# An attention kernel's last batch: output of the batch ahead in an earlier slot, partial products in later slots, a short chunk's products in column blocks

## The chip, the cores and the metric

The kernel runs on one core of a Trainium2 chip. The core has five engines with a queue of instructions each: TensorE (PE, matrix products; its weight loads are shown apart as PEld), VectorE (DVE), ScalarE (ACT), GpSimd (POOL) and SyncE (SP), which issues DMAs. An engine takes its instructions in the order in which the program gives them, and an instruction that waits holds up all behind it on the same engine. DMAs are issued by SP, ACT or POOL and are carried out by 16 DMA engines. The metric is the time of one execution on the device in microseconds (us).

## The reference

The input `x` has 8 batches of 512 features by 1024 tokens, and `cond_2048` is a mask of zeros and ones over the tokens, about half of each. Queries, keys and values are the same projection `q`. The output is `x` plus the attention's result:

```python
xt = jnp.transpose(x, (0, 2, 1))
q = xt @ Wq.T
qh = q.reshape(B, T, NH, dk).transpose(0, 2, 1, 3)
scores = scale * jnp.einsum('bhqd,bhkd->bhqk', qh, qh)
logits = (scores * cmask + (1.0 - cmask) * NEG) * rmask
attn = jax.nn.softmax(logits, axis=-1)
ctx = jnp.einsum('bhqk,bhkd->bhqd', attn, qh)
ctx = ctx.transpose(0, 2, 1, 3).reshape(B, T, D)
out = ctx @ Wo.T
return jnp.transpose(out, (0, 2, 1))      # and x is added to it
```

There are 8 heads of 64 features. `cmask` is the mask over keys, `rmask` over queries. A masked key has no weight. A masked query has all its logits at zero, so its result is the mean of the values of all tokens, the same for every masked query of a batch.

## The kernel before

The kernel computes only with the kept tokens of a batch. `NK` = 544 rows hold the kept tokens and, as the last row, the mean of all tokens, which stands for every masked query. (Were more tokens kept, another version of the same code with 576 rows, or one without the selection, would run; neither does here.) The 544 rows are cut into five chunks: four of 128, and a short one, number `LAST` = 4, of 32 (`END`). `sizes[i]` is a chunk's row count and `places[i]` its rows in the result: the short chunk's are 0 to 31, chunk 0's 32 to 159, and so on.

Work goes by pairs of heads: 4 pairs a batch, 32 in all, written (b, pr) below. The loop over `pairs` (lines 1302 to 1381) writes the order out by hand, in five slots k = 0 to 4 a pair. Each slot takes one chunk of keys, the short one first (`order`, line 1276). In a slot stand, in this order: the chunk's scores (`scores`: products on PE, exponentials on ACT); at slot 0 the contexts of an earlier pair; fetches of an earlier batch (`fetch`, on POOL, each after a tiny copy `keep_step` that reads this slot's exponentials and so holds POOL back until then); the slot's tasks from `slots_of(p)`, which are projections, values, the attention of the pair before, and output products of the batch before; row loads (`load_rows`, on SP); and transposes of an earlier batch (`finish_blocks`, on VectorE). Tables such as `FETCH_LAST` say which pieces go into which (pr, k).

The names that the change touches:

- `output` (line 869) computes a chunk's result for all four pairs, has ACT copy it to `oc`, and stores it from POOL's queue into `od`, a buffer in memory with 544 rows a batch. For the short chunk it uses four column blocks already: the 512 columns are cut into four of 128, and each goes to another 32 partitions of the same bank, so that copy and store have 128 partitions.
- `load_rows`, `fetch` and `finish_blocks` turn that into the output. For each of 8 pieces, `load_rows` loads rows of `x` (turned, in the buffer `xd`) into `g`; `fetch` gathers the matching rows of `od` and has DMA add them to `g`; `finish_blocks` transposes `g` into `xr`. A fetch waits for all stores to the batch's `od`. After the eighth transpose `xr` is stored to the output in four DMAs of 512 KB on SP's queue (line 949). For batches 0 to 5 this happens two batches on; for batch 6, in pairs (7,2) and (7,3).
- `inverses`, `spread`, `contexts`: the reciprocals of the sums of exponentials. `inverses` works them out on VectorE, `spread` brings them to all rows by products on PE and a copy on ACT, and `contexts` multiplies a pair's result `cT` by them on VectorE. For all but the last two pairs, `invert` does the spreading by DMAs (`row`, `rb`).
- The last batch has no batch behind it that could hide its output. `begin_output` (line 893) forms a chunk's product of the first three pairs during the last pair (7,3) and copies it to `pa`. After the loop, `attend_last` ends the last pair, and `end_output` (line 909) adds the fourth pair's product, a chunk at a time, and stores the sum into `od` from SP. Then `fetch_last` gathers eight pieces of 128 tokens on POOL (line 958), and `finish_tokens` transposes each on PE (line 987), adds `x` on VectorE (line 988) and stores 256 KB from ACT's queue. The gather of piece i waits for the stores of the short chunk and of chunks 0 to i.

Of the kernel before, what the change touches and what calls it, by code (L numbers as in the profile page):

```python
# [13 lines left out]
ALU = mybir.AluOpType  # L14
# [292 lines left out]
def attention_of_kept_tokens(ctx, tc, x, mask, wq, wo, out, ident, wqT, woT, verdict, flag):  # L307


    nc = tc.nc  # L310
    B, D, T = x.shape
    P = 128
    DK = D // NH
    SCALE = 1.0 / math.sqrt(DK)
    ND = D // P
# [4 lines left out]
    A = P // Q  # L320
# [570 lines left out]
    partials = {}  # L891

    def begin_output(b, i):

        n = sizes[i]
        po = bank(f"pa_{b}_{i}")
        for pr in range(ND - 1):
            nc.tensor.matmul(
                po[:n, :],
                cTs[b, pr][:, i * P : i * P + n],  # L900
                woT[:, pr, :],
                start=(pr == 0),
                stop=(pr == ND - 2),
            )
        pa = sb.tile([P, D], F32, tag="xin", name=f"pa_{b}_{i}", bufs=NC)
        nc.scalar.copy(pa[:n, :], po[:n, :])
        partials[i] = pa

    def end_output(b, i):
        n = sizes[i]  # L910
        if i == 0:
            ods[b] = dr.tile([NK, D], F32, tag="od", name=f"od_{b}")
        po = bank(f"po_{b}_{i}")
        nc.tensor.matmul(
            po[:n, :],
            cTs[b, ND - 1][:, i * P : i * P + n],
            woT[:, ND - 1, :],
            start=True,
            stop=True,
        )  # L920
        oc = sb.tile([P, D], F32, tag="oc", name=f"oc_{b}_{i}", bufs=NC)
        nc.vector.tensor_tensor(
            oc[:n, :].rearrange("p (d a f) -> p a d f", d=ND, a=A),
            po[:n, :].rearrange("p (a d f) -> p a d f", d=ND, a=A),
            partials[i][:n, :].rearrange("p (a d f) -> p a d f", d=ND, a=A),
            ALU.add,
        )
        nc.sync.dma_start(ods[b][places[i], :], oc[:n, :])

# [71 lines left out]
    def slots_of(p):  # L1001
# [7 lines left out]
        def do(k, f, *args):  # L1009
            todo[k].append(lambda: f(*args))  # L1010
# [60 lines left out]
        elif ahead:  # L1071
            do(1, project_with_values)
            do(2, lengths_of, behind)
            do(2, end_attend, before)
            do(3, project_with_top, 1)
        elif behind:
            do(1, output, b - 1, LAST - 1)
            do(1, values, behind)
            do(2, lengths_of, behind)
            do(2, end_attend, before)  # L1080
            do(3, bias_of, behind)
            do(3, output, b - 1, LAST)
        if p == ND - 1:
# [173 lines left out]
    def late(n):  # L1257
# [39 lines left out]
        FINISH = {(0, 4): (0, 1), (1, 1): (2, 3), (1, 2): (4, 5), (1, 4): (6, 7)}  # L1297
        FETCH_LAST = {(2, 4): (0, 1, 2), (3, 0): (3, 4, 5), (3, 1): (6, 7)}
        FINISH_LAST = {(3, 1): (0, 1, 2), (3, 2): (3, 4, 5), (3, 3): (6, 7)}
        ROWS = {(2, 2): (0, 1), (2, 3): (2, 3), (3, 0): (4, 5), (3, 2): (6, 7)}  # L1300
        ROWS_LAST = {(2, 0): (0, 1, 2), (2, 1): (3, 4, 5), (2, 2): (6, 7)}
        for p, pair in enumerate(pairs):
# [3 lines left out]
            for k, c in enumerate(order):  # L1306
# [78 lines left out]
        attend_last(last)  # L1385
        for i in (0, LAST, *range(1, LAST)):
            end_output(B - 1, i)
# [116 lines left out]
```

## Time and profile before

| | us |
|---|---|
| median of 3 runs | 659.57 |
| lowest and highest | 658.69 to 660.84 |
| the profiled execution | 660.24 |
| its span, first to last instruction | 658.5 |
| PE busy | 618.8 (94%) |
| ACT busy | 383.6 (58%) |
| DVE busy | 355.7 (54%) |
| POOL busy | 212.0 (32%) |
| mean granted TensorE clock | 0.980 |

The profile is of one execution. In its timeline a row has the start in us, the duration, the engine, the line of the kernel, the operation, out<-in by the program's names with shapes, and a count of merged instructions; in square brackets stands the time for which the engine was idle before, and what ended it. A matmul with 32-bit operands shows as two records. In the rows by stretches stand, after the stretch and its length, the busy time and count of PE, PEld, DVE, ACT and POOL, then the granted TensorE clock, the DMA engines' mean busy share, and GB/s.

Pair (7,2) runs in the profiled execution from about 578 to 598 us, pair (7,3) from there to about 620, `attend_last` to 628, the last products to 633, and the gathers and final stores to the end.

### The profile page before, as it was taken

Reading aid. Unit: us, or ns where it says so; the run is one execution under the profiler, and the core shown is the slowest. Engines: PE = TensorE matmul, PEld = TensorE weight load, DVE = VectorE, ACT = ScalarE, POOL = GpSimd, SP = SyncE. Lnnn points to the kernel's source line nnn. Section 1 sums busy time; section 2 is a strip of 40 time slices with the busy share of each in tenths; the row PEclk is TensorE's granted clock in tenths of the full one; section 3 lists DMA queues with packets and bytes.
Section 4 is the critical chain, followed back from the end, with each engine's and each line's share of the span. In section 5 each row is a group of like instructions: output and inputs, shape, how many; then the busy total and the mean of one; then the engine's idle time right before and its main releaser. Section 6 shows DMA issues by size and latency. Waiting matters only on the chain. (4 is left out here: it accounts for less than half of the span.)

```text
span 658.5 us, 15960 instructions
## 1 busy us (share of the span) xinstructions
PE 618.8 (94%) x6092; PEld 383.9 (58%) x6092; DVE 355.7 (54%) x1032; ACT 383.6 (58%) x1020; POOL 212.0 (32%) x313
## 2 busy tenths in 40 slices
PE   5799799999999999999999999999999999998963
PEld 4765476656665666556665666566665666554422
DVE  5545566434475666746475548565665425435542
ACT  4268558755766567754776577655775466553400
POOL 5620500150067003830166004720275006205331
PEclk9999899999999999999999999999999999999975
DMA  8556622354488657977599666975795636477776
GB/s 244 176 199 162 222 69 66 113 193 132 134 177 218 231 176 191 189 242 228 169 180 274 196 189 151 205 249 180 200 174 156 196 102 102 101 178 179 123 219 195
DMA packets 94542, 116.61 MB, mean 177 GB/s; under 512 B 11911, under 2 KB 61639, under 8 KB 94462
## 3 DMA queue, kind: packets, MB, share of 16 engines
q1 hardware_dynamic: 74030, 75.20, 38.6%
q0 software_dynamic: 16208, 38.25, 25.1%
q10 hardware_dynamic: 4224, 2.10, 1.1%
q8 instruction: 49, 0.80, 0.5%
q14 instruction: 31, 0.25, 0.1%
HBM read 72.81 MB, written 42.70 MB: 175 GB/s over the span
## 5 line engine op out<-in xcount | busy, mean ns | idle before, releaser
L687 ACT ACTIVATE e<-s,bias 128x544 f32<-128x544 f32 x256 | 180.5, 710 | 73.6 <-PE s L679 60.2
L679 PE MATMUL s<-qT 64*64 64x272 f32 x2048 | 155.0, 398 | 5.5 <-ACT e L687 3.8
L743 PE MATMUL av<-e,v 64*64 64x272 f32 x1920 | 132.2, 392 | 0.0
L593 PE MATMUL pq<-xc,wqT 128*128 128x272 f32 x512 | 131.3, 401 | 0.0
L593 PEld LDWEIGHTS pq<-xc,wqT 128*128 128x128 f32 x512 | 93.3, 190 | 36.9 <-issue 20.6
L679 PEld LDWEIGHTS s<-qT 64*64 64x64 f32 x2048 | 77.3, 133 | 54.8 <-ACT e L687 12.4
L878 PE MATMUL po<-woT,cT 128*128 128x512 f32 (+1 forms) x448 | 108.9, 439 | 0.0
L889 POOL DMA_DIRECT2D od<-oc x56 | 30.2, 544 | 236.5 <-ACT oc L887 235.7
L972 POOL DMA_INDIRECT g<-od,block_origin x56 | 90.1, 1610 | 29.4 <-DVE ends L716 8.3
L743 PEld LDWEIGHTS av<-e,v 64*64 64x64 f32 x1920 | 76.5, 134 | 38.1 <-issue 2.1
L659 DVE TENSOR_REDUCE m<-pq 128x1 f32<-128x128 f32 x28 | 8.2, 292 | 136.4 <-ACT qT L605 111.9
L878 PEld LDWEIGHTS po<-woT,cT 128*128 128x128 f32 (+1 forms) x448 | 46.5, 149 | 54.6 <-issue 53.2
L603 ACT COPY qT<-pq 128x272 f32<-128x272 f32 x64 | 24.6, 385 | 69.5 <-PE pq L650 28.2
L942 DVE STREAM_TRANSPOSE xr<-g 128x512 f32<-128x512 f32 x56 | 58.0, 1101 | 7.1 <-DMA g<-od,block_origin 7.1
L640 DVE TENSOR_REDUCE len<-sq 128x10 f32<-128x640 f32 x32 | 25.7, 804 | 59.2 <-ACT sq L638 59.2
L969 POOL COPY step<-e 1x1 f32<-1x1 f32 x75 | 24.0, 320 | 96.5 <-ACT e L687 96.4
L687 ACT ACTIVATION_READ_ACCUMULATOR e<-s,bias 128x1 f32 x256 | 50.5, 197 | 0.0
L539 POOL DMA_INDIRECT xin<-xd,source x40 | 39.1, 978 | 16.0 <-DMA woT<-in_L_cond_Wq_dram 5.8
L887 ACT COPY oc<-po 128x512 f32<-128x512 f32 (+1 forms) x35 | 18.0, 515 | 44.0 <-PE po L878 43.1
L493 ACT ACTIVATE junka<-x 128x512 f32<-128x512 f32 x56 | 35.2, 629 | 1.3
L474 DVE STREAM_TRANSPOSE xt<-x 128x1024 f32<-128x1024 f32 x28 | 34.8, 1241 | 0.7 <-issue 0.2
L527 DVE TENSOR_SCALAR_CACHE_REDUCE junk<-rank,key 128x1024 f32<-128x1024 f32 (+4 forms) x35 | 34.9, 997 | 0.0
(174 smaller groups left out, 674.6 us busy)
## 6 DMA issues: line engine op xcount, KB each, us to landing
xd<-xt SPq DMA_DIRECT2D x120, 128.0 KB
x<-in_x_dram SPq DMA_DIRECT2D x56, 256.0 KB
g<-xd SPq DMA_DIRECT2D x56, 256.0 KB
out_dram<-xr SPq DMA_DIRECT2D x28, 512.0 KB
rb<-row SPq DMA_DIRECT2D x60, 160.0 KB
od<-oc POOLq DMA_DIRECT2D x28, 256.0 KB
rank<-ranks SPq DMA_DIRECT2D x6, 512.0 KB
x<-in_x_dram POOLq DMA_DIRECT2D x8, 256.0 KB
```

The lines of the kernel that those rows point to most:

```text
L474: nc.vector.transpose(xt.rearrange("p k (d f) -> p k d f", d=ND), xs[b][r][:, :, at : at + n].rearrange("p d (k t) -> p k d t", t=Q),)
L493: nc.scalar.activation(junk, xs[b][r][:, d, :], AF.Copy, accum_out=xbars[b][:, d, r : r + 1])
L527: nc.vector.tensor_scalar(junk[:, :n], rank[:, i * P :], key[:, col], 0.0, ALU.is_le, ALU.add, accum_out=found[:, col])
L539: nc.gpsimd.indirect_dma_start(out=xin[:n, :], out_offset=None, in_=xds[b], in_offset=bass.IndirectOffsetOnAxis(ap=searches[b][2][:n, i : ...
L593: nc.tensor.matmul(pq[:, :KH], wqT[:, d, pr * P : (pr + 1) * P], xcs[b][:, d, cols], start=(d == 0), stop=(d == ND - 1),)
L679: nc.tensor.matmul(ss[h][r * DK : (r + 1) * DK, hf, :KH], qT[heads[h], c * P + r * DK : c * P + (r + 1) * DK], qT[heads[h], queries[hf]], ...
L687: nc.scalar.activation(e[:, :, h, :], ss[h][:, :, :KH], AF.Exp, bias=bias, scale=SCALE, accum_out=sums[pair[1] % 2][:, h, c : c + 1],)
L743: nc.tensor.matmul(avs[pair][hf][head, :KH], v[keys, c, head], e[keys, hf, h, :], start=(c == 0 and not crossed), stop=(c == LAST - 1 and ...
L878: nc.tensor.matmul(po[k * n : (k + 1) * n, :w], cTs[b, pr][:, i * P : i * P + n], woT[:, pr, k * w : (k + 1) * w], start=(pr == 0), stop=( ...
L889: nc.gpsimd.dma_start(ods[b][places[i], k * w : (k + 1) * w], oc[k * n : (k + 1) * n, :w])
L942: nc.vector.transpose(xr.rearrange("p (d a) (t i) -> p a d t i", a=A, i=NT)[..., i], gs[b, i].rearrange("p (a d f) -> p a d f", a=A, f=Q),)
L972: nc.gpsimd.indirect_dma_start(out=gs[b, i], out_offset=None, in_=ods[b], in_offset=bass.IndirectOffsetOnAxis(ap=block_origin[:, b, i : i ...
```

## The change

Three things change together, all of them around the last batch:

1. In pair (7,2) the last two output products of batch 6, chunks 3 and `LAST`, both go to slot 0 (before: slots 1 and 3). The tables for batch 6 move with them: row loads from slots 0 to 2 of (7,2) to slots 2 to 4 of (7,1) and slot 1 of (7,2); fetches from (7,2) slot 4 and (7,3) slots 0 and 1 to (7,2) slots 2 to 4 and (7,3) slots 0 and 1, at most two a slot; transposes from (7,3) slots 1 to 3 to (7,2) slot 4 and (7,3) slots 1 and 2.
2. In the last pair, `spread` and `contexts` of the pair before go to slot 0 (before: slot 1), and the five partial products to slots 1, 2, 3, 4, 4 (before: 1, 1, 2, 3, 4).
3. The short chunk of the last batch uses four column blocks too, in `begin_output` and `end_output`. The blocks take the columns of `woT` in the final order, so the add needs no reordering for it. It becomes the first chunk of the last five, and its store four DMAs, two each from SP and ACT.

```diff
+    def add_product(b, i, pr, po, start, stop):
+
+        n = sizes[i]
+        parts = P // n
+        w = D // parts
+        tokens = cTs[b, pr][:, i * P : i * P + n]
+        if parts == 1:
+            nc.tensor.matmul(po, tokens, woT[:, pr, :], start=start, stop=stop)
+            return
+        in_order = woT[:, pr, :].rearrange("p (a d f) -> p d a f", a=A, d=ND)
+        for k in range(parts):
+            nc.tensor.matmul(
+                po[k * n : (k + 1) * n, :w],
+                tokens,
+                in_order[:, k * ND // parts : (k + 1) * ND // parts, :, :],
+                start=start,
+                stop=stop,
+            )
+
     def begin_output(b, i):
...
         for pr in range(ND - 1):
...
+            add_product(b, i, pr, po, pr == 0, pr == ND - 2)
+        w = D // (P // sizes[i])
         pa = sb.tile([P, D], F32, tag="xin", name=f"pa_{b}_{i}", bufs=NC)
-        nc.scalar.copy(pa[:n, :], po[:n, :])
+        nc.scalar.copy(pa[:, :w], po[:, :w])
         partials[i] = pa
 
     def end_output(b, i):
...
-        if i == 0:
+        if i == LAST:
             ods[b] = dr.tile([NK, D], F32, tag="od", name=f"od_{b}")
         po = bank(f"po_{b}_{i}")
...
+        add_product(b, i, ND - 1, po, True, True)
         oc = sb.tile([P, D], F32, tag="oc", name=f"oc_{b}_{i}", bufs=NC)
...
+        else:
+            nc.vector.tensor_tensor(oc[:, :w], po[:, :w], partials[i][:, :w], ALU.add)
+        for k in range(parts):
+            queue = nc.scalar if k % 2 else nc.sync
+            queue.dma_start(ods[b][places[i], k * w : (k + 1) * w], oc[k * n : (k + 1) * n, :w])
...
         elif behind:
-            do(1, output, b - 1, LAST - 1)
+            do(0, output, b - 1, LAST - 1)
+            do(0, output, b - 1, LAST)
             do(1, values, behind)
             do(2, lengths_of, behind)
             do(2, end_attend, before)
             do(3, bias_of, behind)
-            do(3, output, b - 1, LAST)
...
             for i in range(NC):
-                do((1, 1, 2, 3, 4)[i], begin_output, b, i)
+                do((1, 2, 3, 4, 4)[i], begin_output, b, i)
...
-        FETCH_LAST = {(2, 4): (0, 1, 2), (3, 0): (3, 4, 5), (3, 1): (6, 7)}
-        FINISH_LAST = {(3, 1): (0, 1, 2), (3, 2): (3, 4, 5), (3, 3): (6, 7)}
+        FETCH_LAST = {(2, 2): (0, 1), (2, 3): (2, 3), (2, 4): (4, 5), (3, 0): (6,), (3, 1): (7,)}
+        FINISH_LAST = {(2, 4): (0, 1), (3, 1): (2, 3, 4), (3, 2): (5, 6, 7)}
         ROWS = {(2, 2): (0, 1), (2, 3): (2, 3), (3, 0): (4, 5), (3, 2): (6, 7)}
-        ROWS_LAST = {(2, 0): (0, 1, 2), (2, 1): (3, 4, 5), (2, 2): (6, 7)}
+        ROWS_LAST = {(1, 2): (0, 1), (1, 3): (2, 3), (1, 4): (4, 5), (2, 1): (6, 7)}
...
-                if p + 1 == len(pairs):
-                    if k == 1:
-                        spread(before, inv)
-                        contexts(before)
+                if p + 1 == len(pairs) and k == 0:
+                    spread(before, inv)
+                    contexts(before)
...
-        for i in (0, LAST, *range(1, LAST)):
+        for i in (LAST, *range(LAST)):
             end_output(B - 1, i)
```

More of the change, by code (lines that the diff above doesn't have):

```diff
@@ L891, in attention_of_kept_tokens @@
     partials = {}
+    def add_product(b, i, pr, po, start, stop):
[15 more added lines that the diff above has]
+            )
     def begin_output(b, i):
-        n = sizes[i]
         po = bank(f"pa_{b}_{i}")
         for pr in range(ND - 1):
[L898 to L904, printed above, removed]
+            add_product(b, i, pr, po, pr == 0, pr == ND - 2)
+        w = D // (P // sizes[i])
         pa = sb.tile([P, D], F32, tag="xin", name=f"pa_{b}_{i}", bufs=NC)
-        nc.scalar.copy(pa[:n, :], po[:n, :])
+        nc.scalar.copy(pa[:, :w], po[:, :w])
         partials[i] = pa
@@ L910, in end_output @@
         n = sizes[i]
-        if i == 0:
+        parts = P // n
+        w = D // parts
+        if i == LAST:
             ods[b] = dr.tile([NK, D], F32, tag="od", name=f"od_{b}")
         po = bank(f"po_{b}_{i}")
[L914 to L920, printed above, removed]
-        oc = sb.tile([P, D], F32, tag="oc", name=f"oc_{b}_{i}", bufs=NC)
[L922 to L928, printed above, removed]
+        add_product(b, i, ND - 1, po, True, True)
+        oc = sb.tile([P, D], F32, tag="oc", name=f"oc_{b}_{i}", bufs=NC)
+        if parts == 1:
+            nc.vector.tensor_tensor(
+                oc.rearrange("p (d a f) -> p a d f", d=ND, a=A),
+                po.rearrange("p (a d f) -> p a d f", d=ND, a=A),
+                partials[i].rearrange("p (a d f) -> p a d f", d=ND, a=A),
+                ALU.add,
+            )
+        else:
[3 more added lines that the diff above has]
+            queue.dma_start(ods[b][places[i], k * w : (k + 1) * w], oc[k * n : (k + 1) * n, :w])
     def in_blocks(t):
```

## The prediction

> **What bounds the kernel now.** I read the page first, then the chain that ended last, then the timeline of the last two pairs and of the tail, then busy time by stretches.
>
> ```profile
> span 658.5 us, 15960 instructions
> PE 618.8 (94%) x6092; PEld 383.9 (58%) x6092; DVE 355.7 (54%) x1032; ACT 383.6 (58%) x1020; POOL 212.0 (32%) x313
> ```
> ```profile
> 644.05 7.22 DMA g<-od,origin
> ...
> 651.40 1.10 PE o L987 x4
> ...
> 652.52 0.69 DVE x L988
> ```
>
> TensorE is busy for 94% of the span, so up to about 633 us a stall or a saving on PE counts one for one. After that PE is nearly empty, and the end hangs on the eight fetches of the last batch (POOL, line 958). Two things therefore set the end: when PE reaches the last products (line 914), and how long after them the first fetch starts.
>
> ```profile
> 620.42 1.12 DVE L942 STREAM_TRANSPOSE xr<-g 128x512 f32<-128x512 f32 x1 [0.60 <-DMA g<-od,block_origin]
> 620.51 1.14 PE L725 MATMUL av<-e,v 128*64 128x272 f32 x8
> 621.39 0.15 DVE L819 SCALAR_TENSOR_TENSOR share<-share,lacks,pads 128x4 f32<-128x4 f32 x1
> 621.56 5.29 SPq L949 DMA_DIRECT2D out_dram<-xr  x4
> 622.53 1.31 PE L805 MATMUL rb<-ident,ris 128*64 128x128 f32 x20 [0.89 <-DVE ris L826]
> 627.88 4.87 PE L914 MATMUL po<-woT,cT 128*128 128x512 f32 x10
> 628.48 0.15 DVE L796 COPY cT<-qT 128x1 f32<-128x1 f32 x1
> 629.77 4.07 SPq L928 DMA_DIRECT2D od<-oc  x5
> 630.02 0.68 DVE L922 TENSOR_TENSOR oc<-po,pa 32x512 f32<-32x512 f32 x1 [0.28 <-PE po L914]
> 635.22 1.00 POOL L958 DMA_INDIRECT g<-od,origin  x1 [19.14 <-DMA od<-oc]
> ```
>
> Batch 6's fetches and transposes (lines 972, 942) run through the last pair. Its last transpose stands on VectorE ahead of the last pair's inverses (line 819 on), so PE waits 0.89 us at the spread (line 805). Then batch 6's output, 4 x 512 KB, is issued on SP at 621.56, and the last batch's od stores queue behind it: the short chunk's add ends at 630.70, and the fetch that needs it and chunk 0 starts at 635.22, 4.5 us later.
>
> **The change part by part.** The sum is made against the profiled execution: 660.24 us, 1.7 over its span and 0.67 over the median of 659.57.
>
> *Short chunk in blocks.* Three matmuls with 512 moving columns become twelve with 128.
>
> ```profile
> 590.93 1.08 PE L878 MATMUL po<-woT,cT 128*32 128x128 f32 x32
> 617.81 2.76 PE L898 MATMUL pa<-woT,cT 128*32 128x512 f32 x6
> ```
>
> The rows count each f32 matmul twice. Line 878 has the blocked form already: 32 records in 1.08 us, 0.034 each. So 24 records cost 0.81 us where the partial product took 2.76: **-1.9 us** of PE (bounds -2.0, and -1.0 if the strided moving operand of line 914's new helper halves the rate). The copy to `pa` shrinks too, but nobody waits for it.
>
> *Order of the last products.* The short chunk now goes first, and it needs the last context column, ready at 628.63; before, chunk 0 ran under that wait. Its 8 records cost some 0.3 us and its 128x128 add some 0.2. By the old clock times: short chunk 628.9 to 629.3, chunk 0 to 630.1, add of chunk 0 630.2 to 630.9. So the later of the two stores that fetch 0 needs is released at 630.9, where it was 630.7: **+0.2** (bounds 0 and +0.8, one SP issue, 4.07 / 5). Of the short chunk's four stores two are on ACT's queue, which is idle there; the two on SP pass before chunk 0's add ends.
>
> *Batch 6's end moved ahead.* Its last six transposes now stand ahead of the inverses by two score blocks and more; by the times worked out below they end near 615, the inverses come near 619, and most of the 0.89 wait goes: **-0.8** (bounds -0.9 and 0). The output stores start there too. The old ones, issued at 621.56, still kept DMA at 0.92 and 0.88 between 630 and 634, some 12.4 us; the new ones are out at about 627.5.
>
> ```profile
> 630.00:632.00 2.00, 2.00 (x5) 0.97 (x6) 1.43 (x3) 0.00 (x0) 0.00 (x0) 1.00 0.92 199
> 632.00:634.00 2.00, 0.76 (x2) 0.01 (x1) 1.67 (x5) 0.00 (x0) 0.00 (x0) 1.00 0.88 274
> ...
> 654.00:656.00 2.00, 0.00 (x0) 0.00 (x0) 0.00 (x0) 0.00 (x0) 0.00 (x0) 0.50 0.49 139
> 656.00:658.50 2.50, 0.00 (x0) 0.00 (x0) 0.00 (x0) 0.00 (x0) 0.00 (x0) 0.50 0.00 0
> ```
>
> The last column but one is the DMA share. The kernel's very last 256 KB store meets empty queues: its add ends at 653.21 and DMA is silent from 656, at most 2.8 us. With 0.3 for POOL to start, the 4.5 us wait becomes 3.1: **-1.4** (bounds -1.9, and 0 if the wait isn't made by the queue). The next fetches don't wait: all adds end within line 914's 4.87 us, and POOL alone takes 1.00 for each fetch.
>
> *Contexts of the pair before at slot 0.* This takes out two PE waits of before (0.81 us for an exponential, 1.28 for the contexts), but only if VectorE delivers. And here the same change puts something in its way. Two of batch 6's transposes now stand at the end of pair (7,2), so on VectorE they are ahead of the contexts and inverses that the spread at slot 0 of (7,3) needs.
>
> ```profile
> 589.00:591.00 2.00, 1.46 (x25) 0.77 (x23) 0.98 (x2) 1.94 (x6) 0.00 (x0) 1.00 0.01 2
> ...
> 595.00:597.00 2.00, 2.00 (x17) 0.97 (x16) 1.72 (x6) 0.39 (x1) 0.00 (x0) 1.00 0.87 288
> ```
> ```profile
> 581.57 3.70 PE L878 MATMUL po<-woT,cT 128*128 128x512 f32 x8
> 581.74 0.71 ACT L687 ACTIVATE e<-s,bias 128x544 f32<-128x544 f32 x1 [1.51 <-PE s L679]
> 592.63 1.98 POOL L889 DMA_DIRECT2D od<-oc  x4 [5.90 <-ACT oc L887]
> 593.83 0.70 ACT L687 ACTIVATE e<-s,bias 128x544 f32<-128x544 f32 x1
> 594.17 0.23 DVE L854 TENSOR_TENSOR rb<-rb 128x64 f32<-128x64 f32 x1 [2.39 <-DMA rb<-row]
> 597.45 0.18 DVE L827 TENSOR_SCALAR ris<-ends,pads 128x2 f32<-128x2 f32 x1
> 599.84 1.13 PE L679 MATMUL s<-qT 64*64 64x272 f32 x12 [0.81 <-ACT el L704]
> 600.90 1.31 PE L805 MATMUL rb<-ident,ris 128*64 128x128 f32 x20
> 600.94 1.70 POOL L972 DMA_INDIRECT g<-od,block_origin  x1 [6.16 <-DVE ends L716]
> 602.94 1.58 POOL L972 DMA_INDIRECT g<-od,block_origin  x1 [0.25 <-issue]
> 605.40 3.70 PE L898 MATMUL pa<-woT,cT 128*128 128x512 f32 x8 [1.28 <-DVE cT L862]
> 605.85 1.11 DVE L942 STREAM_TRANSPOSE xr<-g 128x512 f32<-128x512 f32 x1 [0.31 <-DMA g<-od,block_origin]
> 608.14 1.11 DVE L942 STREAM_TRANSPOSE xr<-g 128x512 f32<-128x512 f32 x1 [1.18 <-DMA g<-od,block_origin]
> ```
>
> When is that spread, S, now? Batch 6's last products move to slot 0 of (7,2): they start a score block (1.1 us) earlier than 581.57, at 580.6, and end after 3.70 + 1.08 at 585.4; as before, 0.6 us later POOL issues the short chunk's four stores for 1.98, to 588.0. The first fetch needs them landed. Before, it started 6.3 us after their issue ended (594.61 to 600.94), but with DMA at 0.87 from other loads; the bound below is the 2.8 + 0.3 of the quiet store. The new place, 588 to 591, is quiet (0.01 at 589), because the row loads (line 936) have moved into pair (7,1), so I take the near end: fetch 0 at 591.1, fetch 1 two us on at 593.1. Fetches land 4.9 (600.94 to 605.85) and 5.2 us after their start; with `rb` and two row loads beside them, I take 5.5: fetch 1 is in at 598.6. Then one transpose, 1.1, contexts and inverses, 3.5 (594.17 to 597.63), and 0.1 to start: **S = 603.3** where it was 600.90. Bounds: 602.7, all of it quiet, and 606.8, with the 6.3 and a landing of 5.8.
>
> What runs behind S is as long as before: the partial products wait for the contexts 4.5 us after the spread starts (605.40 - 600.90), and spread 1.31, one score block 1.1 and two products 1.7 lie below that. So the term is S - 600.90 = **+2.4**, the two old waits included. VectorE ends the contexts at 607.8, adds the ends (1.0) and does the six transposes (6.7): 615.5. PE begins the last attention at 620.51 + 2.4 - 1.9 = 621.0; the exponentials that the inverses need lie a partial product (2.8 or less) before.
>
> *Filler lost in (7,2).* Both products now lie ahead of the score blocks, where they no longer cover the exponentials. The first exponential moves from 581.74 to about 586.6; four pairs of them at 1.5, the copies and the square (2.1) and some 1.3 of waits for scores bring the last one to 596.0 instead of 594.53. So PE is free for the spread at 600.4, not 599.0 (599.84 - 0.81): +1.4 (bounds 0 and +2.7), which lies wholly under the wait until 603.3, and costs itself if that wait is gone. SP only gains: six row loads now pass before batch 5's output (576.4), where VectorE, not the queue, is what that output waits for; two stay behind the `rb` loads. The other queue, POOL's, holds nothing but fetches there.
>
> Sum: +2.4 - 1.9 - 0.8 + 0.2 - 1.4 = -1.5, that is S - 604.8. 658.7 for the profiled execution, **658.1** as a median: a gain of 0.2%, inside the 0.3% (2 us) in which a measurement of this kernel can't tell a change from none.
>
> One thing speaks against it, the granted clock (third column from the end), here early in the span and after the last product:
>
> ```profile
> 70.00:75.00 5.00, 1.83 (x25) 0.91 (x17) 4.49 (x20) 0.83 (x3) 3.99 (x7) 1.00 0.73 224
> 75.00:80.00 5.00, 4.91 (x48) 2.54 (x48) 1.64 (x6) 3.59 (x9) 3.33 (x4) 0.66 0.38 134
> ...
> 631.95:635.36 3.41, 1.08 (x3) 0.08 (x1) 2.29 (x8) 0.00 (x0) 0.14 (x1) 1.00 0.92 314
> 635.37:638.00 2.63, 0.00 (x0) 0.00 (x0) 0.00 (x0) 0.00 (x0) 2.02 (x3) 0.50 0.38 134
> ```
>
> In the lower rows PE was busy for 1.08 of 3.41 us, and the clock fell from 1.00 to 0.50. In the upper ones PE was busy for 1.83 of 5 us, and then the mean was 0.66 over 5 us, that is half the clock for (1 - 0.66) / 0.5 x 5 = 3.4 us. The new wait at the spread is 603.3 - 600.4 = 2.9 us, nearly as empty. [...]
>
> **The rivals.**
> 1. *The hold on VectorE is short.* If the fetches land so early that S is between 600.4 (PE's own pace) and 602.8, the time is 655.2 to 657.6; middle 656.4. For it: the queues are empty at 589. Against: it needs fetch 1 landed by 598.1, under the bound from the rows.
> 2. *The hold is long; slower.* If fetch 0 again starts 6.3 us after the short stores, S is 606.8 and the time 661.6; with half a clock behind it up to 663.3. It decides from S = 604.8, fetch 1 landed at 600.1. For it: that is the only such wait which the trace has. Against: the loads that filled DMA then are gone.
> 3. *The clock falls in the hold.* 3.4 us at half the clock cost PE at most 1.7: 659.8. [...]
> 4. *The first fetch gains nothing from empty queues.* Then -1.4 falls away: 659.5. For it: the DMA share of 0.92 may only be coincident with a slow store. Against: the stores stand on one queue, in order.
>
> **How the numbers follow.** Forecast 0.37, rivals 0.25, 0.16, 0.14, 0.08. The forecast's own range is 657.5 to 659.5. Faster is rival 1 and the forecast's lower edge, 0.29; slower is rival 2 and a part of 3, 0.21; within 0.3% is the rest, 0.50. As cases of both signs hold 0.41, the range goes from rival 1's lower end to the middle of rival 2: 655.2 to 662.6.
>
> **What would show it.** Right: a PE wait of 2 to 4 us on `ris` before line 805 at slot 0 of the last pair, behind two line-942 transposes that wait for their fetches; fetch 0 of batch 6 at 590 to 592; the short chunk's partial product under 1 us; no wait before the second spread; batch 6's output issued near 615; the first line-958 fetch about 3 us after chunk 0's add, and 23.3 us from it to the end, as before (635.22 to 658.5). Wrong: a spread at 601 or at 606, a partial product still over 2 us, a clock of 0.50 in the last pair, a first fetch still 4.5 us behind, or exponentials of (7,2) that end after 598.

## The result, and the profile after

| | before, us | after, us |
|---|---|---|
| median, on the same chip | 659.7 | 661.36 |
| lowest to highest | 655.87 to 661.56 | 659.3 to 663.06 |
| the profiled execution | 660.24 | 661.35 |
| its span | 658.5 | 659.6 |

The ratio of after to before is **1.0028**, with a 95% interval of 1.0014 to 1.0041: the change makes the kernel a little slower, by 0.9 to 2.7 us. The forecast was 1.5 us faster.

The page of the changed kernel, first its span and busy times; then, from the chain that ended last (start, duration, what it was), the stretch ahead of the spread at slot 0 of the last pair.

```profile
span 659.6 us, 16022 instructions
PE 619.5 (94%) x6116; PEld 386.2 (59%) x6116; DVE 353.6 (54%) x1032; ACT 384.1 (58%) x1020; POOL 212.4 (32%) x313
```
```profile
588.80 3.14 DMA od<-oc
592.89 7.90 DMA g<-od,block_origin
606.10 2.40 PE rb L805 x20
```

The busy times are nearly those of before, but in this stretch the chain doesn't run over PE (the chain in the profile of before goes back only to 641.23 us and can't be laid beside it). It runs through the stores of batch 6's last chunk and its first fetch before it comes back at the spread. The timeline around these rows and after (line 956 is the old 942, 963 the old 949, 972 the old 958, 986 the old 972, 900 the products in one piece and 904 those in blocks, 932 and 939 the two adds):

```profile
556.79 0.72 ACT L704 ACTIVATE el<-s,bias 128x544 f32<-128x544 f32 x1
587.31 1.99 POOL L889 DMA_DIRECT2D od<-oc  x4 [0.17 <-issue]
592.28 1.09 SPq L844 DMA_DIRECT2D rb<-row  x2
592.89 1.70 POOL L986 DMA_INDIRECT g<-od,block_origin  x1 [1.54 <-DMA od<-oc]
593.47 1.01 SPq L950 DMA_DIRECT2D g<-xd  x2
594.89 1.58 POOL L986 DMA_INDIRECT g<-od,block_origin  x1 [0.25 <-issue]
596.01 0.71 ACT L687 ACTIVATE e<-s,bias 128x544 f32<-128x544 f32 x1
600.82 2.02 DVE L956 STREAM_TRANSPOSE xr<-g 128x512 f32<-128x512 f32 x2 [6.25 <-DMA g<-od,block_origin]
606.10 2.40 PE L805 MATMUL rb<-ident,ris 128*64 128x128 f32 x20 [4.78 <-DVE ris L826]
618.18 5.28 SPq L963 DMA_DIRECT2D out_dram<-xr  x4
624.60 0.86 PE L904 MATMUL pa<-woT,cT 128*32 128x128 f32 x24
625.39 1.14 PE L725 MATMUL av<-e,v 128*64 128x272 f32 x8
626.36 1.26 PE L805 MATMUL rb<-ident,ris 128*64 128x128 f32 x20
633.04 0.29 DVE L939 TENSOR_TENSOR oc<-po,pa 128x128 f32<-128x128 f32 x1 [0.63 <-PE po L904]
634.07 0.69 DVE L932 TENSOR_TENSOR oc<-po,pa 128x512 f32<-128x512 f32 x1 [0.74 <-PE po L900]
637.69 1.00 POOL L972 DMA_INDIRECT g<-od,origin  x1 [24.10 <-DMA od<-oc]
```

PE stands idle for 4.78 us before the spread at slot 0 of the last pair (L805, 606.10), because VectorE stands idle for 6.25 us before its first transpose of batch 6, and that waits for fetch 0. Busy time by stretches (columns as before; granted clock third from the end) shows what follows:

```profile
604.00:606.00 2.00, 0.00 (x0) 0.00 (x0) 1.67 (x8) 0.00 (x0) 1.78 (x1) 0.50 0.94 149
606.00:608.00 2.00, 1.90 (x18) 1.90 (x20) 0.20 (x2) 0.00 (x0) 0.23 (x1) 0.50 0.88 126
608.00:610.00 2.00, 2.00 (x22) 0.90 (x18) 0.98 (x4) 0.76 (x2) 0.00 (x0) 0.50 0.54 85
610.00:612.00 2.00, 2.00 (x12) 0.87 (x5) 1.90 (x8) 1.50 (x4) 0.23 (x1) 0.99 0.00 0
```

The clock is halved in the wait, and PE works at 0.50 for four more microseconds: the spread takes 2.40 us where it took 1.31, the score block behind it 1.91 where it takes 1.15 at full clock, in no_hold and pe_kept_busy below.

To compare places in the two traces I count from one instruction ahead of all that is changed, the first exponential of the short chunk in pair (7,1). It stands at 556.79 here and stood in the profile before in this row:

```profile
555.47 0.72 ACT L704 ACTIVATE el<-s,bias 128x544 f32<-128x544 f32 x1
```

So "on the clock of before" means less 1.32 us. This offset is there in the first 40 us already (the first square, line 638, begins at 35.95 in the profile before and at 37.12 here), and it goes the other way in the second pair of profiles (36.47 before, 34.94 after); it is scatter and not the change.

### The profile page after: what moved, and what is told of

Read it like the earlier page. It is cut to its first block, busy times and chain, and to the rows that moved or that the text cites. A ratio compares the mean times of both kernels' runs of the same rounds, so it can differ in the third digit from the quotient of the medians.

```text
span 659.6 us, 16022 instructions
## 1 busy us (share of the span) xinstructions
PE 619.5 (94%) x6116; PEld 386.2 (59%) x6116; DVE 353.6 (54%) x1032; ACT 384.1 (58%) x1020; POOL 212.4 (32%) x313
## 4 chain that ended last, share of the span: by engine, by line
PE 81%; issue 6%; DMA 4%; DVE 3%; ACT 3%; POOL 1%; SPq 1%; another core or an unknown queue 1%; POOLq 0%; DVEq 0%; ACTq 0%
PE s L679 19%; PE pq L593 18%; PE av L743 15%; PE po L878 14%; PE s L701 3%; PE xc L552 3%; PE av L725 3%; PE pa L900 2%; ACT e L687 2%; PE v L621 2%; DMA g<-od,block_origin 1%; PE warm L432 1%; DMA x<-in_x_dram 1%; DMA g<-od,origin 1%; DMA woT<-in_L_cond_Wq_dram 1%
```

## The experiments

They were made on three chips, whose level differs by about 1%, so every ratio is to the kernel before on the same chip.

| run | median us | before, same chip | ratio, 95% interval |
|---|---|---|---|
| before_again | 653.15 | 653.49 | 1.0008 (0.9991 to 1.0025) |
| after_again | 655.91 | 653.49 | 1.0035 (1.0019 to 1.0051) |
| no_hold | 649.24 | 653.49 | 0.9945 (0.9924 to 0.9966) |
| rows_first | 655.59 | 653.49 | 1.0041 (1.0023 to 1.0060) |
| no_hold_no_blocks | 656.60 | 658.90 | 0.9964 (0.9949 to 0.9980) |
| early_undone | 659.40 | 658.90 | 1.0010 (0.9994 to 1.0026) |
| pe_kept_busy | 658.95 | 658.90 | 0.9996 (0.9976 to 1.0017) |
| no_hold_slot1 | 653.55 | 658.90 | 0.9909 (0.9887 to 0.9932) |
| slot1_again | 654.76 | 660.29 | 0.9911 (0.9886 to 0.9936) |
| slot1_old_order | 653.84 | 660.29 | 0.9898 (0.9874 to 0.9923) |
| one_hold | 659.24 | 660.29 | 0.9986 (0.9966 to 1.0006) |
| part1_only | 660.64 | 660.29 | 1.0011 (0.9995 to 1.0027) |

The theory after the result: the hold (VectorE waiting for batch 6's first two fetches ahead of the inverses) is longer than forecast and halves the clock besides. Its rival: the loss is elsewhere, in the blocks, the order or the tail.

The diffs are against the kernel after, unless another is named. In the second table each profile is cut at the same instructions: from the reference exponential to the spread S (line 805), from there to the last attention (line 725), to the second spread, to the end of the later of the two adds that the first gather waits for, to that gather, and to the end of the span. All in us.

| profile | to S | to attention | to 2nd spread | to add | to gather | to end | sum |
|---|---|---|---|---|---|---|---|
| before | 45.43 | 19.61 | 2.02 | 8.17 | 4.51 | 23.30 | 103.04 |
| before_again | 45.42 | 19.14 | 1.24 | 8.17 | 4.51 | 23.21 | 101.70 |
| after | 49.31 | 19.29 | 0.97 | 8.41 | 2.92 | 21.93 | 102.83 |
| after_again | 49.57 | 19.22 | 0.97 | 8.41 | 2.92 | 22.25 | 103.34 |
| no_hold | 44.47 | 17.44 | 0.97 | 8.41 | 2.93 | 21.77 | 95.98 |
| rows_first | 49.29 | 19.53 | 0.97 | 8.41 | 3.49 | 21.67 | 103.36 |
| no_hold_no_blocks | 44.46 | 19.37 | 0.97 | 9.00 | 2.81 | 22.27 | 98.88 |
| early_undone | 43.47 | 17.44 | 5.87 | 9.82 | 3.83 | 21.36 | 101.79 |
| pe_kept_busy | 49.13 | 17.43 | 0.97 | 8.41 | 2.92 | 21.90 | 100.76 |
| no_hold_slot1 | 43.70 | 17.44 | 0.97 | 8.41 | 2.93 | 22.35 | 95.80 |
| slot1_again | 43.70 | 17.58 | 0.97 | 8.41 | 2.92 | 23.34 | 96.92 |
| slot1_old_order | 43.70 | 17.49 | 0.97 | 7.35 | 3.55 | 23.45 | 96.52 |
| one_hold | 48.87 | 19.05 | 0.97 | 8.41 | 2.92 | 22.17 | 102.39 |
| part1_only | 49.30 | 20.02 | 0.97 | 8.12 | 2.42 | 23.20 | 104.02 |

### before_again and after_again: both kernels unchanged

> The kernel before, once more, as the null of this comparison: ratio 1.000. Its profile says whether the 1.2 us by which the changed kernel was late after its first 40 us (36 us into the span, in both traces the same instructions) is scatter. Theory 'start is scatter': the first square of the first pair (ScalarE, line 638; 35.95 us before, 37.12 after) lies anywhere between 35.5 and 37.5 here. Theory 'start belongs to the change': it lies at 35.9 to 36.2 again.

> The changed kernel, once more: ratio 1.001 to 1.004. Theory 'hold': PE again waits 4 to 5.5 us for the inverses before line 805 at slot 0 of the last pair, and the granted clock falls to 0.50 in or behind that wait. Theory 'start belongs to the change': the first square of the first pair is again at 37.0 to 37.3; by 'start is scatter' it may be anywhere between 35.5 and 37.5.

The first gives 1.0008 with an interval that includes 1; the second 1.0035. The small loss is there on a second chip, and so is its shape: S comes 4.15 us later than in the run of before, behind a wait of 5.04 us.

### no_hold: the two transposes leave pair (7,2)

```diff
-        FINISH_LAST = {(2, 4): (0, 1), (3, 1): (2, 3, 4), (3, 2): (5, 6, 7)}
+        FINISH_LAST = {(3, 1): (0, 1, 2, 3, 4), (3, 2): (5, 6, 7)}
```

> The changed kernel with one edit: the first two transposes of batch 6 move from slot 4 of pair (7,2) to slot 1 of the last pair, behind the contexts. Theory 'hold' (these two transposes keep VectorE, so the spread starts at 606.1 where PE is free at 601.3, and the clock is halved for 6.8 us behind it): the spread starts at PE's pace, 601.5 to 602 by the changed kernel's clock times, no clock of 0.50 before the tail; 4.3 us from the wait and 1 to 1.7 from the clock: 655 to 656.5, ratio to before 0.993 to 0.995. Theory 'filler' (the products moved to slot 0 of (7,2) no longer cover the exponentials, and that is what costs): at most 1 us less than the changed kernel, 660 to 661. Theory 'start belongs to the change': 1.2 us above what 'hold' gives, 656.5 to 658.

0.9945, that is 6.7 us less than the kernel after on the same chip and 4.25 less than before. The timeline of this run:

```profile
594.12 0.84 PE L701 MATMUL s<-qT 64*64 64x272 f32 x6
594.88 1.31 PE L805 MATMUL rb<-ident,ris 128*64 128x128 f32 x20
596.13 1.15 PE L679 MATMUL s<-qT 64*64 64x272 f32 x16
599.82 3.90 DVE L956 STREAM_TRANSPOSE xr<-g 128x512 f32<-128x512 f32 x4
```

The spread follows the short chunk's scores without a gap and at full speed, and the transposes, now behind it, don't wait. S is 5.1 us earlier than in after_again, the way from S to the last attention 1.8 us shorter: together 6.9, about the difference of the times. Moving two entries of a table turns the loss into a gain, so the loss lies in those two transposes. The rival falls.

### pe_kept_busy: the wait stays, the clock doesn't fall

```diff
                 if p + 1 == len(pairs) and k == 0:
+                    warm(28, ident)
                     spread(before, inv)
```

This adds 28 transposes of the identity on PE, whose results nobody reads, to fill PE's wait.

> The changed kernel with 28 transposes of the identity on PE, whose results nobody reads, ahead of the spread at slot 0 of the last pair: some 4.2 us of work in a wait of 4.8. The wait for VectorE stays as long. Theory 'the clock costs beside the wait': no clock of 0.50 before the tail, the spread's 20 records take 1.3 in place of 2.4 us, and the time falls by 1.4 to 1.9 from the changed kernel's: ratio to before 1.000 to 1.002. Theory 'the clock costs nothing there, since what follows waits for VectorE anyway': unchanged, ratio 1.003 to 1.005.

Its timeline, and behind it its busy time by stretches:

```profile
601.27 3.27 PE L432 MATMUL warm<-ident 128*128 128x128 f32 x28
605.93 1.31 PE L805 MATMUL rb<-ident,ris 128*64 128x128 f32 x20 [1.39 <-DVE ris L827]
607.17 1.15 PE L679 MATMUL s<-qT 64*64 64x272 f32 x16
```
```profile
602.00:606.00 4.00, 2.61 (x26) 2.40 (x26) 3.48 (x13) 0.21 (x2) 3.44 (x5) 1.00 0.94 143
606.00:610.00 4.00, 4.00 (x40) 2.23 (x41) 1.98 (x6) 2.25 (x6) 0.66 (x1) 1.00 0.73 116
```

The 28 transposes took 3.27 us; the 4.2 expected was the author's estimate. S is where it is in after (49.13), but the clock stays at 1.00 and the way to the last attention is 17.43 us instead of 19.2 to 19.3. The time is that of before, 0.9996, where after has 1.0028 and 1.0035. So of the 6.7 us between after and no_hold, about 1.8 are the clock's and about 5 the wait's own.

### rows_first: the last two row loads out of the fetches' way

```diff
-        ROWS_LAST = {(1, 2): (0, 1), (1, 3): (2, 3), (1, 4): (4, 5), (2, 1): (6, 7)}
+        ROWS_LAST = {(1, 2): (0, 1), (1, 3): (2, 3), (1, 4): (4, 5)}
...
                         finish_blocks(b - 2, i)
+                if b + 1 == B and (pr, k) == (1, 4):
+                    load_rows(b - 1, 6)
+                    load_rows(b - 1, 7)
```

> The changed kernel with one edit: the last two row loads of batch 6 stand at the end of slot 4 of pair (7,1), ahead of batch 5's output on SP, in place of slot 1 of (7,2). In the changed kernel no packet of the first fetch moves between 593 and 597, while these loads and rb move, and its landing comes 7.9 us after its start. Theory 'the loads hold the fetch': first fetch lands 5 to 6 us after its start, the spread starts at 603.5 to 604.5 by the changed kernel's clock times, and the time falls by 1.6 to 3.5: 658 to 659.8. Theory 'the fetch is slow by itself there' (its own start, not the loads): landing again 7 to 8 us after start, time unchanged, 661 to 661.7.

The time doesn't change: 1.0041 beside 1.0035. But the parts of the wait do. Its timeline:

```profile
587.72 1.70 POOL L986 DMA_INDIRECT g<-od,block_origin  x1 [2.67 <-DVE top L647]
589.72 1.58 POOL L986 DMA_INDIRECT g<-od,block_origin  x1 [0.25 <-issue]
593.05 1.11 DVE L956 STREAM_TRANSPOSE xr<-g 128x512 f32<-128x512 f32 x1 [4.78 <-DMA g<-od,block_origin]
595.44 1.10 DVE L956 STREAM_TRANSPOSE xr<-g 128x512 f32<-128x512 f32 x1 [1.28 <-DMA g<-od,block_origin]
599.79 2.40 PE L805 MATMUL rb<-ident,ris 128*64 128x128 f32 x20 [4.76 <-DVE ris L826]
```

The DMA queues from 2.1 to 4.1 us after fetch 0 starts (packets, MB, share of 16 engines; q0 carries the fetches, q1 what SP issues), in the kernel after:

```profile
q1 hardware_dynamic: 219, 0.41, 85.2%
q0 software_dynamic: 1, 0.00, 0.6%
```

And at the same distance in rows_first:

```profile
q0 software_dynamic: 91, 0.19, 69.8%
q1 hardware_dynamic: 52, 0.09, 14.2%
```

Without the row loads beside them, the fetches land 5.3 us (593.05 - 587.72) and 5.7 us after they start, where fetch 0 of the kernel after took 7.9. So the two row loads (593.47) did delay it; SP's `rb` loads stand beside the fetch in both runs. The delay isn't one number: in the five profiles that have both the hold and the row loads, fetch 0 took 7.1 to 8.1 us, but in no_hold, with the same loads, 6.3.

In rows_first, however, fetch 0 starts 1.1 us later, counted from the reference instruction (37.2 us instead of 36.1), and now it is fetch 1 that holds up VectorE: it lands at 44.9, and its transpose ends at 46.0, as the second transpose does in after. So the spread comes out at the same place. The likely reason for the late start is that the row loads, now ahead of batch 5's output on SP, push what follows them into the stores of batch 6's chunks, for which the fetch waits: in the 3.6 us after the issue of these stores, SP's queue takes 21.3% of the DMA engines here and 5.6% in after. (The idle time is put down to VectorE, but no fetch needs that instruction.) No run shows this apart.

### one_hold: one transpose stays

```diff
-        FINISH_LAST = {(2, 4): (0, 1), (3, 1): (2, 3, 4), (3, 2): (5, 6, 7)}
+        FINISH_LAST = {(2, 4): (0,), (3, 1): (1, 2, 3, 4), (3, 2): (5, 6, 7)}
```

> The changed kernel with one transpose of batch 6 in slot 4 of (7,2) in place of two. Theory 'hold': the spread starts after the first fetch's landing, one transpose and the chain of contexts and inverses, 1.0 to 1.3 us sooner than in the changed kernel; the wait of PE is 3.5 to 4 us and the clock falls once or twice more: 1 us less than the changed kernel, ratio to before 1.001 to 1.0025; without the fall of the clock 0.9985 to 1.000. Theory 'any transpose before the contexts costs the same': ratio 1.003 to 1.0045.

The timeline of this run:

```profile
600.24 1.10 DVE L956 STREAM_TRANSPOSE xr<-g 128x512 f32<-128x512 f32 x1 [6.47 <-DMA g<-od,block_origin]
604.81 2.32 PE L805 MATMUL rb<-ident,ris 128*64 128x128 f32 x20 [4.33 <-DVE ris L826]
```

One transpose is enough for nearly the whole wait, since it is fetch 0 that comes late: S is 0.4 to 0.7 us sooner than in after. The time is 0.9986, 3 us under what after showed on the other chips and also less than was expected. Its own profile accounts for 0.4 to 1.0 of these (102.39 beside 102.83 and 103.34), of which a part is the clock, which falls for one window of 3.41 us here and for two in after; the rest stays open.

### part1_only: batch 6 moved, all else as before

Against the kernel before:

```diff
-            do(1, output, b - 1, LAST - 1)
+            do(0, output, b - 1, LAST - 1)
+            do(0, output, b - 1, LAST)
...
-            do(3, output, b - 1, LAST)
...
-        FETCH_LAST = {(2, 4): (0, 1, 2), (3, 0): (3, 4, 5), (3, 1): (6, 7)}
+        FETCH_LAST = {(2, 2): (0, 1), (2, 3): (2, 3), (2, 4): (4, 5), (3, 0): (6,), (3, 1): (7,)}
...
```

(`FINISH_LAST` and `ROWS_LAST` as in the kernel after, too.)

> The kernel before with the change's first part alone: batch 6's last products in slot 0 of (7,2), its row loads, fetches and transposes earlier; spread at slot 1, partial products and the short chunk as before. Theory 'the hold is in the first part': VectorE is held up as long as in the changed kernel, PE waits 2.5 to 3.5 us before the spread and again 1 to 1.5 for the contexts; 3.8 us lost there, 0.8 won at the second spread and 1.4 at the first fetch, up to 1.5 lost to the clock: 1.6 to 3.1 us above before, ratio 1.002 to 1.005. Theory 'the hold comes from the spread in slot 0': the score block at slot 0 covers it, and the part alone gains 1 to 2 us, ratio 0.997 to 0.9985.

1.0011, with an interval that includes 1. The spread, still at slot 1, has a wait of 2.80 us, and the clock falls for one window of 3.41 us:

```profile
605.04 2.40 PE L805 MATMUL rb<-ident,ris 128*64 128x128 f32 x20 [2.80 <-DVE ris L826]
```
```profile
603.00:605.00 2.00, 0.00 (x0) 0.00 (x0) 1.74 (x9) 0.37 (x2) 1.85 (x2) 0.97 1.02 143
605.00:607.00 2.00, 1.96 (x18) 1.96 (x20) 0.92 (x5) 0.00 (x0) 1.74 (x3) 0.50 0.95 135
607.00:609.00 2.00, 2.00 (x9) 0.93 (x6) 1.05 (x4) 0.75 (x2) 0.03 (x1) 0.67 0.79 125
```

The ratio is under the expected 1.002 to 1.005, so the time alone doesn't show a loss; the profile shows the wait. So the hold comes with the first part alone; S, counted from the reference instruction, is where it is in after (49.30).

### early_undone: the other two parts without it

```diff
-            do(0, output, b - 1, LAST - 1)
-            do(0, output, b - 1, LAST)
+            do(1, output, b - 1, LAST - 1)
...
+            do(3, output, b - 1, LAST)
...
-        FINISH_LAST = {(2, 4): (0, 1), (3, 1): (2, 3, 4), (3, 2): (5, 6, 7)}
+        FINISH_LAST = {(3, 1): (0, 1, 2), (3, 2): (3, 4, 5), (3, 3): (6, 7)}
```

(`FETCH_LAST` and `ROWS_LAST` as in the kernel before, too.)

> The changed kernel with its first part undone: batch 6's products back in slots 1 and 3 of (7,2), and its row loads, fetches and transposes where they were; the spread at slot 0, the later partial products and the column blocks stay. Theory 'batch 6 is the wall': PE gets to the last attention some 3.5 us sooner, and waits there for the inverses behind batch 6's last transposes, which come when they came before; so PE waits 3 to 5 us before the second spread, maybe with the clock halved, and the time is that of before or up to 1.5 us more: ratio 1.000 to 1.003. Theory 'the parts add up, each for itself': 3.5 us less than before, ratio 0.994 to 0.996.

1.0010: no gain. The timeline shows where the gain goes:

```profile
616.96 1.14 PE L725 MATMUL av<-e,v 128*64 128x272 f32 x8
620.65 1.09 DVE L956 STREAM_TRANSPOSE xr<-g 128x512 f32<-128x512 f32 x1 [0.58 <-DMA g<-od,block_origin]
621.77 5.28 SPq L963 DMA_DIRECT2D out_dram<-xr  x4
622.83 2.40 PE L805 MATMUL rb<-ident,ris 128*64 128x128 f32 x20 [4.74 <-DVE ris L827]
```

PE is at the last attention 4.1 us earlier than before (43.47 + 17.44 against 45.43 + 19.61), without a hold, but then waits 4.74 us at the second spread, behind batch 6's last transpose, whose fetches come when they always came. The clock falls there too, for one window of 3.41 us (the spread takes 2.40 us). What the one stage gains, the next gives back. The earlier fetches are what makes the other two parts worth anything.

### no_hold_no_blocks: the blocks alone

On top of no_hold, the short chunk's products in one piece again (one product with 32 partitions and 512 columns, one store), the order unchanged:

```diff
...
+        nc.tensor.matmul(po[:n, :], tokens, woT[:, pr, :], start=start, stop=stop)
+        return
...
-        nc.scalar.copy(pa[:, :w], po[:, :w])
+        nc.scalar.copy(pa[:n, :], po[:n, :])
...
-        for k in range(parts):
-            queue = nc.scalar if k % 2 else nc.sync
-            queue.dma_start(ods[b][places[i], k * w : (k + 1) * w], oc[k * n : (k + 1) * n, :w])
+        nc.sync.dma_start(ods[b][places[i], :], oc[:n, :])
```

> The kernel without the hold (transposes 0 and 1 of batch 6 in slot 1 of the last pair), and besides the short chunk's products as before, in one piece of 32 rows; its place as first of the last five stays. Theory 'blocks are worth their PE time': the partial product takes 2.76 in place of 0.86 us, the last one 0.87 in place of 0.42 and its add 0.68 in place of 0.29; the first two lie on PE's path, so 2.0 to 2.7 us above the kernel without the hold (649.2), 651.2 to 652, ratio to before 0.996 to 0.998. Theory 'all the gain is in batch 6 being out of the way': within 0.6 us of the kernel without the hold, ratio 0.994 to 0.9955.

0.9964 beside no_hold's 0.9945; the two intervals overlap. From S to the last attention the profiles have 19.37 and 17.44 us: 1.93 us, for the partial product alone, and another 0.6 up to the add (9.00 against 8.41). So the size comes from the profiles.

### no_hold_slot1, slot1_again and slot1_old_order: a better kernel, and the order

The forecast had 1.4 us for the cover that pair (7,2) loses when both products lie at slot 0. Without the hold that should cost itself. On top of no_hold:

```diff
-            do(0, output, b - 1, LAST - 1)
-            do(0, output, b - 1, LAST)
+            do(1, output, b - 1, LAST - 1)
+            do(1, output, b - 1, LAST)
...
-        FETCH_LAST = {(2, 2): (0, 1), (2, 3): (2, 3), (2, 4): (4, 5), (3, 0): (6,), (3, 1): (7,)}
+        FETCH_LAST = {(2, 3): (0, 1), (2, 4): (2, 3, 4), (3, 0): (5, 6), (3, 1): (7,)}
```

> The kernel without the hold, with batch 6's last two products in slot 1 of (7,2) in place of slot 0, and its fetches one slot later (from slot 3 on). Theory 'filler': the first score block's exponentials run under these products again, the last exponential of (7,2) ends 0.5 to 0.9 us sooner than without this edit, and as much is gained: 648.3 to 648.8, ratio 0.993 to 0.9938. Theory 'filler is free': the same as without the edit, 649.2. If the fetches then land too late for the transposes, a wait of 1 us or more appears on VectorE before the second inverses and the time rises to 650 or more.

0.9909. S comes 0.8 us sooner than in no_hold (43.70 against 44.47). The time fell by more than that, from 0.9945 to 0.9909 or some 2.4 us, but on another chip and with intervals that overlap; only the 0.8 is accounted for. slot1_again is the same kernel on another chip; slot1_old_order runs chunk 0 ahead of the short chunk, as the kernel before does:

```diff
-        for i in (LAST, *range(LAST)):
+        for i in (0, LAST, *range(1, LAST)):
```

> The fastest kernel so far (no hold, batch 6's last products in slot 1) once more, beside the next run on the same chip: ratio to before 0.989 to 0.993.

> The kernel of the run beside it with the last five chunks in the old order, chunk 0 ahead of the short one, still in blocks. Theory 'the order costs' (the prediction's +0.2: the short chunk waits for the last context column and chunk 0 behind it): the two stores that the first fetch needs are released 0.6 to 0.9 us sooner after the last context column, and the time falls by 0.2 to 0.9 us against the run beside it. Theory 'the order shortens the tail' (from the first fetch's start to the end of the span there were 23.3 and 23.2 us in the two profiles of before, 21.4 to 22.4 in all eight kernels with the short chunk first): the tail is 23.2 again and the time rises by 0.3 to 1.0 us.

0.9911 and 0.9898. The gain of 0.9% holds on both chips. For the order the intervals overlap nearly wholly, so the times don't settle it. The profiles have the add 1.06 us sooner in the old order (7.35 against 8.41) and the gather then only 0.43 sooner (3.55 us behind the add instead of 2.92).

## Why the prediction was wrong, step by step

The terms of the sum, and what the two pairs of profiles show for them (after less before, after_again less before_again):

| term | forecast | first pair | second pair |
|---|---|---|---|
| contexts at slot 0: S | +2.4 | +3.9 | +4.1 |
| short chunk in blocks: S to last attention | -1.9 | -0.3 | +0.1 |
| batch 6's end ahead: second spread | -0.8 | -1.05 | -0.3 |
| order of the last products: to the add | +0.2 | +0.24 | +0.24 |
| batch 6's end ahead: add to first gather | -1.4 | -1.6 | -1.6 |
| gather to end | 0 | -1.4 | -1.0 |
| sum | -1.5 | -0.2 | +1.6 |
| median of the timed runs | -1.5 | +1.7 | +2.4 |

The measured 661.36 lies inside the forecast's range of 655.2 to 662.6; what came out the other way is the sign. The rest of the sum fits no_hold in total: with PE's own pace (600.4) put in for S, the forecast's S - 604.8 gives -4.4 us, and no_hold measured -4.25.

- **The step that failed is the landing in "Contexts of the pair before at slot 0".** Its mechanism was right: two transposes of batch 6 wait for their fetches, the inverses stand behind them, PE waits. So were the starts: the short chunk's stores end at 589.30, that is 588.0 on the clock of before, as forecast; fetch 0 starts at 591.57 (591.1), fetch 1 at 593.57 (593.1). But the forecast took 5.5 us for a landing, from rows of 4.9 and 5.2, and set the upper bound at 5.8. Fetch 0 took 7.9. The `rb` and row loads were known to be there, and priced at 0.3 to 0.6 us; the row loads alone cost 2.2 to 2.6 us, against the 5.3 and 5.7 of rows_first (1.0 in no_hold, where nothing waits for the fetch). The forecast also had fetch 1 land last, with one transpose behind it; it was fetch 0, at 599.5 on the clock of before, with both transposes behind it, so the contexts began at 601.4 instead of 599.7. S became 604.78 on the clock of before instead of 603.3, by coincidence the 604.8 that the forecast named as the point where gain turns into loss.
- **Rival 3 came on top, and with more than it had.** The wait of 4.78 us left PE at half clock from 603.21 to 610.03, which took back about 1.8 us between S and the last attention (pe_kept_busy 17.43, after 19.29). The forecast priced one window of 3.4 us, at no more than 1.7; there were two. It gave this 0.14, yet the clock fell in waits that don't fill 3.41 us: in after when PE had been idle for 1.9 us, and in part1_only's wait of 2.80 us too (the last section has the rows). The forecast's own formula with the measured S and the clock's 1.7 gives about +1.7, which is the first measured difference; but that agreement is partly luck, since the second spread and the tail came out differently too.
- **Rival 2 has nearly the right number, 661.6, for another reason.** It had fetch 0 starting 6.3 us behind the stores; it started 3.6 us behind them (589.30 to 592.89).
- **Blocks: right.** 24 records in 0.86 us (forecast 0.81), so the strided operand of the bound -1.0 didn't halve the rate, and 1.93 us of PE between no_hold and no_hold_no_blocks. The saving can't be seen in after against before, only because the clock's loss lies in the same stage.
- **Second spread: right in kind.** The wait is gone (0.97 from attention to spread in all kernels that fetch early). What it was worth depends on before, whose own stage is 2.02 in one profile and 1.24 in the other, so its size is less certain than the forecast's -0.8 suggests. Batch 6's output is issued at 616.86 on the clock of before (forecast 615), later by what S is later.
- **Add to first gather: right**, -1.6 for -1.4; this stage is 2.4 to 3.6 us (forecast 3.1) in the kernels whose batch 6 is out earlier, 4.51 in both profiles of before, and 3.83 in early_undone, whose output is issued at 621.77 as before. Rival 4 falls. In part1_only, which moves batch 6 and nothing else, it is 2.42. **Order: right by the profiles**, +0.24, as the sum of two larger parts: slot1_old_order shows that with blocks the order alone costs 1.06 us up to the add and 0.43 up to the gather, and the blocks make up for most of it.
- **Gather to end: assumed rigid at 23.3, and it was not.** It is 21.9 and 22.25 in the two profiles of after. But one and the same kernel (no_hold_slot1, slot1_again) shows 22.35 and 23.34, so a single profile tells this stage only to about 1 us. Whether the change shortens it stays open.
- **Cover lost in (7,2): right to hide under the hold.** The last exponential begins 0.9 us later on the clock of before (596.01 less 1.32, against 593.83), with 1.4 forecast; with the hold gone, putting the products back at slot 1 gains 0.8 us.

The sums of the stages in the first pair of profiles miss the timed difference by 1.9 us, in the second by 0.8: single executions scatter, and only the larger terms (S, the clock, the block product, the first gather) are shown by runs of their own.

## What to carry to other kernels

Work that waits for a transfer should not stand on an engine ahead of something short that the bounding engine waits for: here two transposes of 1.1 us each, moved two slots too far ahead, cost 6.7 us of a 650 us kernel, and moving only them further back made the change a gain. When a fetch is moved into a new place, price its landing with the loads that share that place (fetch 0 took 7.9 us beside them in after, 5.3 without in rows_first), not with the best rows of a quiet one, and price a PE wait like these with the half clock that may follow: in the 3.41 us ahead of each fall here PE was busy for at most 1.53 us, and with 2.02 the clock stayed. A change in several parts is judged by undoing them one at a time: here neither the first part alone, with its hold, nor the other two parts without it gained anything, while all three without the hold gained 0.6%, and 0.9% with the products one slot later. The first part without its hold was not run by itself.

## What the runs showed of the hardware

- The fetches on POOL's queue stood nearly still while loads that SP issued passed: from 595 to 597 us of the kernel after SP's queue took 85.2% of the DMA engines and the fetches' queue 0.6%, one packet, 2.1 us and more after fetch 0 had started. In rows_first the fetches had 69.8% at that same distance from their start. The trace doesn't show whether the fetch's packets were ready in these 2 us, so what kept them back stays open.
- The clock fell for whole windows of 3.41 us: one in part1_only, one_hold and early_undone, two in after (603.21 to 610.03), after_again (596.14 to 602.97) and rows_first. After's clock changes early in the span too, at 77.55 and 80.97 us, and at 640.75 in the tail; with 603.21 and 610.03, these times lie 1, 153, 2 and 9 times 3.413 us apart. The length of PE's wait doesn't tell how many: 4.74 us cost early_undone one window, 4.76 us cost rows_first two. How long PE was busy in a window fits all six. In the 3.41 us just ahead of the fall it was busy for 0.00 (early_undone), 0.14 (one_hold), 0.75 (part1_only), 0.97 (rows_first), 1.42 (after_again) and 1.53 us (after). In pe_kept_busy, the emptiest window on such a grid (counted back in steps of 3.413 us from its next change of clock, at 637.28) has 2.02, and the clock stayed. A first window at half clock with PE busy for 0.37 to 1.10 us was followed by a second; one with 2.83 us or more, by full clock. Two windows of after, and that one of pe_kept_busy (columns as before, PE's busy time behind the length):

```profile
599.80:603.21 3.41, 1.53 (x17) 0.49 (x12) 2.33 (x5) 1.20 (x3) 2.89 (x5) 1.00 0.96 154
603.21:606.62 3.41, 0.52 (x6) 0.52 (x8) 2.61 (x10) 0.00 (x0) 2.76 (x3) 0.50 0.93 145
```
```profile
603.15:606.56 3.41, 2.02 (x25) 1.81 (x25) 2.42 (x9) 0.00 (x0) 2.56 (x3) 1.00 0.98 147
```

The fall in after didn't take an idle window: PE was busy for 1.53 us of the 3.41 ahead of it, 45%.
